# The products of the cosine transform between two halves of convolution 1's multiply-adds

## The chip, the core and the metric

The kernel runs as one program on one core of a Trainium2 chip. The core has a matrix engine (TensorE, "PE" in the profile, with its weight loads shown as "PEld"), a vector engine (VectorE, "DVE"), an engine for activations and copies (ScalarE, "ACT"), GpSimdE ("POOL", which here issues most DMAs and some memsets) and SyncE ("SP", which issues a few DMAs). Each engine works through its own list of instructions in order, and engines wait for each other through semaphores. The metric is the time of one execution in device microseconds.

## The reference

Two layers follow each other on eight images of 32 channels and 128 x 128 pixels. In layer 0 every pixel gets the eight best of 25 shifted copies of the normalised image, chosen by the squared difference summed over a patch. The stack of 256 channels goes through three pairs of a 1x1 convolution and a depthwise 3x3 convolution, and beside that through a small cosine transform (`dct`). The sigmoid of the third pair is multiplied with the transform, and two more 1x1 convolutions bring the product back to 32 channels. Layer 1 normalises again and convolves every channel with one 5x5 kernel.

```python
xb = _patch_match_stack(x)                       # [8, 256, 128, 128]
dct = _conv(xb, dct_w, groups=C)
h = jax.nn.relu(_conv(_conv(xb, w1), w2, groups=CK, pad=1))
h = jax.nn.relu(_conv(_conv(h, w3), w4, groups=CK, pad=1))
wiener = jax.nn.sigmoid(_conv(_conv(h, w5), w6, groups=CK, pad=1))
filt = _conv(wiener * dct, inv_dct_w, groups=C)
x = x + _conv(filt, agg_w)                       # layer 0, on the normalised x
x = x + conv5x5(_gn(x))                          # layer 1
```

## The kernel before

An image is worked through in 17 steps of eight rows (`NS` is 16, and the last step is short). The 256 channels are two halves of 128 partitions. For both halves TensorE does the 1x1 convolution. The depthwise part is split: the first half is done by TensorE with small diagonal weights (`depthwise_t`, tile `pw`, L751), the second half by VectorE as nine multiply-adds over shifted rows (`depthwise_v`). Of these nine, the first is a scaled copy on ScalarE (L722) and the other eight are instructions of VectorE, each `128x1024` (L725). ScalarE ends them with the ReLU or the sigmoid (L729).

The main loop goes over the steps `s`, and in each step over four passes `i` in the order 3, 2, 1, 0. Passes 3, 2 and 1 serve convolution 3, 2 and 1, each for another step (convolution 1 is the youngest). Pass 0 ends the step that convolution 3 has just finished: `final_dct` computes the cosine transform on TensorE into four PSUM tiles `pc` (L810, two pairs, one for rows 0 to 3 and one for rows 4 to 7) from the gathered stack `xf`, and VectorE multiplies them into the result of convolution 3 (L818, four products). In the next step's pass 3, `final_add` does the last 1x1 convolutions (`pa`, L831), VectorE adds the image (`xr`, L839), and GpSimdE issues the stores (`x1d`, L844).

TensorE, VectorE and ScalarE keep the order in which the program calls them (`manual_schedule` with `ORDERED`). `depthwise_v` is a generator, and each `next` on it issues one piece: the scaled copy; the eight multiply-adds; the activation; the move of the two border rows (`rows_before_v`, L655 and L657). The middle of a pass issues the multiply-adds of its own convolution with `next(new_v, None)` (L1094). The activation follows in the next pass with `next(dv, None)` (L1102), and the border rows in the pass after that (`next(kept, None)`, L1097). So in pass 1 VectorE does the eight multiply-adds of convolution 1, and the first thing that it does in pass 0 are the four products; then come the tasks that `tick` releases, and in pass 3 of the next step `xr` and the multiply-adds of convolution 3. ScalarE does convolution 1's ReLU in pass 0, behind the squares `df` that the tasks have brought, and before the first copies `tv` (L678) and the scaled copy L722 of convolution 3.

Tasks are the work on the next image and on layer 1. They are generators that name the engine they want next and a cost; `tick` hands out VectorE's by a budget per pass that is fixed in the program. The tasks of this page are: the differences `df` (L444, squared by ScalarE in L452, summed by TensorE into `pd`, L459), the search for the best eight, `mx` and `idx` (L536, L537), the places `oc` (L551 to L560, transposed by TensorE as `pi`, L569), the transposed costs `pt` and their copy `ct` (L525, L529), and layer 1's normalised rows `xm` (L897) with the matmuls on them (L924, called `p5` in the text, `p` in the profile).

PSUM tiles for the 1x1 convolutions (`pv` L670, `p` L694), `pg`, `pa`, `pc`, `pi`, `pt` and `p5` all come from one pool of five buffers (`ps_x`). A tile can be written only when the reader of its buffer's last tile is done: for `pc` that is the product on VectorE, for `pv` the copy `tv` on ScalarE, for `pa` the addition `xr` on VectorE, for `pg` the copy `xb` (L638) on ScalarE. Which buffer a tile gets, and the order of SyncE's and GpSimdE's instructions, is decided by the framework when the program is built, from its own estimate of when things end. The gather's selection masks `sel` (L616, L617) are ScalarE's.

Of the kernel before, what the change touches and what calls it, by code (L numbers as in the profile page):

```python
# [44 lines left out]
def bm3d_conv_preact(  # L45
# [165 lines left out]
    def push(task):  # L211
        want = next(task, None)
        if want:
            which, cost, *wait = want
            queues[which].append((cost, task, now[0] + (wait[0] if wait else 0)))
# [150 lines left out]
    def prep(b):  # L366

        xn = load_image(b, nc.gpsimd) if b else first
        yield "P", 0
        yield "D", 5.5  # L370
        st = work.tile([P, 8, 6], F32, name=f"st_{b}", tag="st")
        for i in range(8):
            nc.vector.bn_stats(
                st[:, i], xn[:, 3 + 4 * i : 7 + 4 * i, 2 : 2 + W]
            )
        mv = work.tile([P, 2], F32, name=f"mv_{b}", tag="mv")
        nc.vector.bn_aggr(mv, st.rearrange("p a b -> p (a b)"))
        yield "A", 0
        nc.scalar.copy(xn[:, :, 0:2], xn[:, :, 2:3].to_broadcast([P, HR, 2]))
        nc.scalar.copy(  # L380
            xn[:, :, 2 + W :], xn[:, :, 1 + W : 2 + W].to_broadcast([P, HR, 2])
        )
        mr = yield from group_stats(mv, f"a{b}")
        nc.vector.tensor_scalar(
            xn, xn, mr[:, 0:1], mr[:, 1:2], op0=ALU.subtract, op1=ALU.mult
        )
        push(sources(b, xn))

        idx = work.tile([P, 4, 8, K, 4], U32, name=f"idx_{b}", tag="idx", bufs=1)

        sq = dram.tile([NO // 2, 4, HR - 2, HX], F32, name=f"sq_{b}", tag="sq")
        for i in range((HR - 2) // SR):
            pd = ps_d.tile([P, SR // 2, HX], F32, name=f"pd_{b}_{i}", tag="pd")

            for aa in ((2, 4), (0, 0), (1, 1), (3, 2), (4, 3), (5, 5)):
                yield "D", PAIR
                push(squares(b, i, pd, xn, aa, sq, idx))
# [254 lines left out]
    def rows_before_v(i, b, n):  # L652
        v = tv[i - 1]
        if n < NS:
            nc.sync.dma_start(v[:, 0:2], v[:, R : R + 2])  # L655
        else:
            nc.gpsimd.memset(v[:, 0 : i + 1], 0.0)  # L657
# [53 lines left out]
    def depthwise_v(i, b, n):  # L711
        v = tv[i - 1]
        nr = R if n < NS else i
        out_ = accp.tile([P, R, W], F32, name=f"acc{i}_{b}_{n}_1", tag=f"acc{i}1")
        acc = out_[:, :nr]
        for k, (dy, dx) in enumerate(
            ((1, 1), (0, 0), (0, 1), (0, 2), (1, 0), (1, 2), (2, 0), (2, 1), (2, 2))
        ):
            tap = dwv[:, i - 1, 3 * dy + dx : 3 * dy + dx + 1]
            rows = v[:, dy : dy + nr, dx : dx + W]  # L720
            if k == 0:
                nc.scalar.activation(acc, rows, AF.Copy, scale=tap)  # L722
                yield out_
            else:
                nc.vector.scalar_tensor_tensor(  # L725
                    acc, rows, tap, acc, op0=ALU.mult, op1=ALU.add
                )
        yield
        nc.scalar.activation(acc, acc, funcs[i - 1])  # L729
        yield  # L730
        rows_before_v(i, b, n)
# [64 lines left out]
    def final_dct(b, n, acc, xf, j0, j1):  # L796

        for r0 in range(0, R, 4):
            a, z = max(r0, j0), min(r0 + 4, j1)
            if a >= z:  # L800
                continue


            pc = [
                ps_x.tile([P, 4, W], F32, name=f"pc_{b}_{n}_{m}_{r0}", tag="x") for m in range(2)
            ]
            for h in range(2):
                for m in range(2):
                    o = 64 * ((h + m + 1) % 2)
                    nc.tensor.matmul(  # L810
                        pc[m][o : o + 64, : z - a],
                        ldct[64 * h : 64 * h + 64, m],
                        xf[64 * h : 64 * h + 64, m, a:z],
                        start=True,
                        stop=True,
                    )
            for m in range(2):
                nc.vector.tensor_mul(acc[m][:, a:z], acc[m][:, a:z], pc[m][:, : z - a])  # L818
# [179 lines left out]
    def unit(stage, u, *rest):  # L998
        if 0 <= u < len(units) and units[u]:
            if stage is gather_load:  # L1000
                at = (units[u][0], units[u][1] % 8 // 2)
                until(lambda: at in ready, 4.0)
            stage(*units[u], *rest)
# [20 lines left out]
    def turn(credit):  # L1024
        now[0] += 1
        run("D", credit)
        run("A")
        run("P")
        run("Q")

    def until(cond, credit):
        while not cond():
            turn(credit)

    with tc.manual_schedule(engines=ORDERED):
        push(prep(0))
        push(weights())
        push(mixes())
        xbd[0] = dram.tile([P, 2, H, W], F32, name="xbd_0", tag="xbd")
        for i in range(3):  # L1040
            nc.gpsimd.memset(tb[i][0:64, 0], 0.0)
        for u in range(7):
            unit(gather_load, u)

            for _ in range({2: 3, 3: 1}.get(u, 0)):
                turn(4.0)
            unit(gather_select, u - 2)
            unit(gather_pixels, u - 3)
        u = 4

        dt = dv = kept = iter(())

        later = iter(())

        for s in range(len(steps) + 2):
            if s < len(steps):
                b, n = steps[s]
                if s == 2:
                    push(bands())
                if n == (0 if b else 4) and b + 1 < NB:  # L1060
                    until(lambda: b in ready, 4.0)
                    push(prep(b + 1))
                if n == NS - 1 and b + 1 < NB:
                    until(lambda: b + 1 in ready, 4.0)
                    xbd[b + 1] = dram.tile([P, 2, H, W], F32, name=f"xbd_{b+1}", tag="xbd")
            for i in (3, 2, 1, 0):
                si = s - (i - 1 if i else 2)
                live = 0 <= si < len(steps)
                new_v = new_t = iter(())
                if live:  # L1070
                    bi, ni = steps[si]

                if live and i:
                    src = source(i, bi, ni)
                    pointwise_v(i, bi, ni, lws[i - 1], src)
                    new_v, new_t = depthwise_v(i, bi, ni), depthwise_t(i, bi, ni)
                    accs[i, bi, ni] = [None, next(new_v)]
                next(later, None)
                if live and not i:
                    if ni == 0:  # L1080
                        x1d[bi] = dram.tile([C, H, W], F32, name=f"x1d_{bi}", tag="x1d")
                        stats[bi] = work.tile([P, NS + 1, 6], F32, name=f"stat_{bi}", tag="stat")
                    xr, xf, j0, j1 = fins.pop(si)
                run("P")
                if live and not i:
                    final_dct(bi, ni, accs[3, bi, ni], xf, j0, j1)

                run("Q")
                if s < len(steps):
                    unit(gather_select, u + 1, (0,))  # L1090
                    unit(gather_load, u + 3)
                    tick(b, i)
                next(later, None)
                next(new_v, None)  # L1094
                if live and i:
                    pointwise_t(i, bi, ni, lws[i - 1], src)
                next(kept, None)  # L1097
                if s < len(steps):
                    unit(gather_pixels, u)
                next(dt, None)  # L1100
                run("A")
                next(dv, None)  # L1102
                if s < len(steps):
                    unit(gather_select, u + 1, (1,))
                    u += 1
                next(dt, None)
                kept, dv, dt = dv, new_v, new_t
                if live and not i:
                    later = end(bi, ni, xr, j0, j1)
                if not i and 0 <= s - 1 < len(steps):  # L1110
                    fins[s - 1] = final_load(*steps[s - 1])
        next(kept, None)
        for _ in later:
            pass
        until(lambda: {(NB - 1, 0), (NB - 1, 1)} <= done, 4.0)
# [62 lines left out]
```

## Time and profile before

| | |
|---|---|
| median of 3 runs | 6632.68 us (6631.27 to 6632.92) |
| profiled execution | 6624.95 us |
| its span | 6623.2 us |
| mean granted TensorE clock | 0.98 |
| TensorE, VectorE, ScalarE busy | 94%, 89%, 76% of the span |
| one multiply-add of VectorE, 128x1024 | 1284 ns mean, 3072 of them |
| one product of VectorE, 128x512 | 680 ns mean, 496 of them |

The profile is of one execution, and all durations below are from it. A timeline row gives the start in microseconds from the span's start, the time that the row's instructions take together, the engine, the line of the program, the operation, the tiles (written from read), their shapes, the number of instructions, and in brackets the idle time of the engine just before with what ended it. A row of the list of waits gives who waited, behind whom, the total in microseconds, how often, and the longest. A wait for several things is put down to the one that came last.

### The profile page before, as it was taken

What the parts mean: (1) busy time and instruction counts of PE and PEld (TensorE: products, weight loads), DVE (VectorE), ACT (ScalarE), POOL (GpSimd) and SP (SyncE); (2) the same over time, 40 slices, a digit from 0 to 9 for tenths busy, and PEclk for the clock granted to TensorE, in tenths of its full rate; (3) what the DMA queues carried; (4) which work ended last, traced back from release to release, by engine and by line L of the source; (5) the groups of instructions that cost most, each with busy time, mean ns of one, the idle gap of its engine ahead of it and who ended that gap; (6) DMA issues with size and microseconds to landing.
All of it is one profiled execution on the core that took longest, in us unless ns stands there. A gap on an engine that the chain in (4) does not pass through costs nothing.

```text
span 6623.2 us, 234197 instructions
## 1 busy us (share of the span) xinstructions
PE 6230.9 (94%) x102306; PEld 3213.3 (49%) x102306; DVE 5861.9 (89%) x8828; ACT 5052.8 (76%) x6698; POOL 3083.0 (47%) x5015
## 2 busy tenths in 40 slices
PE   5898899999999999999999999999999999999997
PEld 1444455544554445544555544554445544465553
DVE  7899988999889998898989998899888999888786
ACT  5787778777787777877778877887768777687782
POOL 8354446444364343643446444464335543334334
PEclk8899999999999999999999999999999999999998
DMA  4555555655555564555645546465555555456553
GB/s 85 127 138 131 133 129 133 150 132 139 130 145 138 130 147 120 148 135 134 145 121 146 149 127 148 119 155 136 128 139 130 147 137 135 122 140 150 139 132 84
DMA packets 544959, 886.20 MB, mean 134 GB/s; under 512 B 248880, under 2 KB 312944, under 8 KB 543936
## 3 DMA queue, kind: packets, MB, share of 16 engines
q0 software_dynamic: 383648, 611.87, 36.8%
q1 hardware_dynamic: 157776, 258.11, 16.1%
q8 instruction: 805, 13.19, 0.9%
q10 hardware_dynamic: 2512, 1.25, 0.1%
q14 instruction: 218, 1.79, 0.1%
HBM read 420.60 MB, written 216.49 MB: 96 GB/s over the span
## 4 chain that ended last, share of the span: by engine, by line
PE 45%; DVE 29%; ACT 9%; DMA 6%; POOL 6%; issue 4%; SPq 0%; ACTq 0%; POOLq 0%; DVEq 0%
DVE acc L725 20%; PE pw L751 15%; PE pv L670 11%; PE p L694 10%; PE pg L631 4%; POOL xtd L424 2%; DVE idx L537 2%; PE pc L810 2%; ACT df L452 2%; ACT sel L616 2%; DVE df L444 2%; DMA xf<-xbd 1%; DVE acc L818 1%; DMA t<-t 1%; PE p L924 1%
## 5 line engine op out<-in xcount | busy, mean ns | idle before, releaser
L725 DVE SCALAR_TENSOR_TENSOR acc<-tv,dwv,acc 128x1024 f32<-128x1024 f32 (+3 forms) x3264 | 4032.3, 1237 | 237.7 <-ACT acc L722 133.7
L751 PE MATMUL pw<-t,dwd 96*32 96x254 f32 (+7 forms) x31680 | 2119.7, 419 | 23.3 <-DMA t<-t 15.2
L751 PEld LDWEIGHTS pw<-t,dwd 96*32 96x32 f32 (+1 forms) x31680 | 1079.7, 110 | 851.3 <-issue 386.1
L616 ACT ACTIVATE sel<-ib,nplace 128x1024 f32<-128x1024 uint8 x1024 | 1172.5, 1145 | 32.2 <-DMA ib<-idxd 32.2
L617 ACT ACTIVATE sel<-sel 128x1024 f32<-128x1024 f32 x1024 | 1085.9, 1060 | 32.5
L694 PE MATMUL p<-acc,lw 128*32 128x256 f32 x16768 | 1006.7, 383 | 26.5 <-ACT tv L678 26.5
L670 PE MATMUL pv<-acc,lw 128*32 128x512 f32 x8448 | 956.2, 590 | 52.0 <-DVE acc L818 46.7
L602 POOL DMA_DIRECT2D ib<-idxd x512 | 292.4, 571 | 1242.3 <-ACT sel L616 1186.9
L791 POOL DMA_DIRECT2D xf<-xbd x1088 | 652.6, 629 | 310.7 <-PE pc L810 176.1
L694 PEld LDWEIGHTS p<-acc,lw 128*32 128x32 f32 x16768 | 575.1, 112 | 444.4 <-issue 81.3
L452 ACT ACTIVATE df<-df 128x786 f32<-128x786 f32 (+2 forms) x576 | 468.6, 861 | 348.4 <-DVE df L444 345.8
L631 PE MATMUL pg<-sel,xt 120*32 120x88 f32 (+1 forms) x24576 | 618.8, 244 | 66.8 <-ACT sel L617 51.4
L631 PEld LDWEIGHTS pg<-sel,xt 120*32 120x32 f32 x24576 | 557.9, 111 | 238.4 <-ACT sel L617 69.9
L678 ACT COPY tv<-pv 128x512 f32<-128x512 f32 (+2 forms) x784 | 436.8, 580 | 296.6 <-PE pv L670 283.8
L444 DVE TENSOR_TENSOR df<-xn 128x786 f32<-128x786 f32 (+2 forms) x576 | 531.6, 973 | 86.0 <-PE pd L459 84.9
L729 ACT ACTIVATE acc<-acc 128x1024 f32<-128x1024 f32 (+3 forms) x408 | 417.3, 1023 | 240.8 <-DVE acc L725 240.5
L764 ACT ACTIVATE acc<-pw 128x512 f32<-128x512 f32 (+2 forms) x808 | 438.4, 573 | 167.2 <-PE pw L751 165.8
L670 PEld LDWEIGHTS pv<-acc,lw 128*32 128x32 f32 x8448 | 284.2, 111 | 538.8 <-issue 426.6
L701 ACT COPY t<-p 128x512 f32<-128x512 f32 x800 | 424.2, 572 | 119.8 <-PE p L694 119.7
L722 ACT ACTIVATE acc<-tv,dwv 128x1024 f32<-128x1024 f32 (+3 forms) x408 | 454.9, 1115 | 33.0 <-PE pa L831 19.1
L670 PE MATMUL pv<-xb,lw 128*32 128x512 f32 x4096 | 471.1, 593 | 0.0
L694 PE MATMUL p<-xb,lw 128*32 128x256 f32 x8192 | 468.1, 379 | 0.2 <-DVE xy L936 0.2
(155 smaller groups left out, 5923.1 us busy)
## 6 DMA issues: line engine op xcount, KB each, us to landing
ib<-idxd POOLq DMA_DIRECT2D x512, 256.0 KB, 4.1
xbd<-xb POOLq DMA_DIRECT2D x128, 1024.0 KB, 5.8
xf<-xbd POOLq DMA_DIRECT2D x960, 128.0 KB, 6.9
t<-t SPq DMA_DIRECT2D x792, 128.0 KB
t<-t SPq DMA_DIRECT2D x384, 256.0 KB
tv<-tv SPq DMA_DIRECT2D x384, 130.0 KB
xt<-xtd POOLq DMA_DIRECT2D x240, 180.0 KB, 3.8
xtd<-xl POOLq DMA_DIRECT2D x192, 96.0 KB, 3.4
```

Source lines behind the costliest of these rows:

```text
L444: nc.vector.tensor_sub(df[:, :, ca:cz], xn[:, r0 : r0 + SR, ca:cz], xn[:, r0 + dy : r0 + dy + SR, ca + dx : cz + dx],)
L452: nc.scalar.activation(df[:, :, ca:cz], df[:, :, ca:cz], AF.Square)
L616: nc.scalar.activation(sel, ib, AF.Square, bias=nplace)
L617: nc.scalar.activation(sel, sel, AF.Relu, scale=-1.0, bias=1.0)
L631: nc.tensor.matmul(pg[C * j : C * (j + 1), :, :, xa:xz], xt[: 8 * QW, f * (NT // 2) + t], sels[j // 2][: 8 * QW, j % 2 * 2 : j % 2 * 2 + 2 ...
L670: nc.tensor.matmul(ps[C * j : C * (j + 1), :hr], lhsT[:, g, P + C * j : P + C * (j + 1)], src(g)[:, h : h + hr], start=g == 0, stop=g == 1,)
L694: nc.tensor.matmul(ps[C * r : C * (r + 1), e, :nb], lhsT[:, g, s], rows[:, r : r + 4 * nb - 3 : 4], start=g == 0, stop=g == 1,)
L722: nc.scalar.activation(acc, rows, AF.Copy, scale=tap)
L725: nc.vector.scalar_tensor_tensor(acc, rows, tap, acc, op0=ALU.mult, op1=ALU.add)
L751: nc.tensor.matmul(pt[u][C * j : C * (j + 1), ka:kz, :nb, xa:xz], dwd[0:hi, i - 1, u, j, dx + 1], t[0:hi, j, ka:kz, :nb, xa + dx : xz + dx ...
L764: nc.scalar.activation(rows[:, u : u + 2 * nh[u] - 1 : 2, :nb], pt[u][:, : nh[u], :nb], funcs[i - 1])
L791: nc.gpsimd.dma_start(xf[p : p + C, m, j0:j1], src[g, m, (h + m + 1) % 2, :, :, ya:yz])
```

## The change

The eight multiply-adds of convolution 1 are issued in two pieces. The generator stops once more before the fifth of them, for convolution 1 alone, and pass 0 calls for the second piece right after `final_dct`. So VectorE's order becomes: four multiply-adds, four products, four multiply-adds. The order of TensorE's and ScalarE's instructions stays as it was. No instruction is added or removed.

```diff
@@ depthwise_v @@
                 nc.scalar.activation(acc, rows, AF.Copy, scale=tap)
                 yield out_
             else:
+                if i == 1 and k == 5:
+                    yield
                 nc.vector.scalar_tensor_tensor(
                     acc, rows, tap, acc, op0=ALU.mult, op1=ALU.add
                 )
@@ main loop @@
                 run("P")
                 if live and not i:
                     final_dct(bi, ni, accs[3, bi, ni], xf, j0, j1)
+                if not i:
+                    next(dv, None)
 
                 run("Q")
```

The taps are issued in the order (1,1), (0,0), (0,1), (0,2), (1,0), (1,2), (2,0), (2,1), (2,2), and `k` counts them from 0, so the second piece holds the last four.

## The prediction

> **What bounds the kernel now.** First the page's engines and the chain that ended last, then the list of waits, then timelines of single blocks.
>
> ```profile
> PE 6230.9 (94%) x102306; PEld 3213.3 (49%) x102306; DVE 5861.9 (89%) x8828; ACT 5052.8 (76%) x6698; POOL 3083.0 (47%) x5015
> ...
> PE 45%; DVE 29%; ACT 9%; DMA 6%; POOL 6%; issue 4%; SPq 0%; ACTq 0%; POOLq 0%; DVEq 0%
> ```
>
> No engine bounds it alone: the chain changes hands between TensorE and VectorE. The waits (microseconds in total, times, longest) name the hand-overs:
>
> ```profile
> ACT df L452 <- DVE df L444: 345.8, 89, 11.4
> ...
> ACT acc L729 <- DVE acc L725: 240.5, 91, 6.1
> DVE xr L839 <- PE pa L831: 228.4, 54, 8.1
> ...
> DVE acc L725 <- ACT acc L722: 133.7, 124, 4.7
> ...
> PE pv L670 <- DVE acc L818: 46.7, 25, 3.0
> ...
> PE p L694 <- ACT tv L678: 26.5, 12, 3.7
> ```
>
> TensorE's 46.7 us behind the products (L818) are what earlier products can free: `pv` waits for a PSUM buffer that `pc` holds. The 240.5 and 345.8 us are ScalarE waiting for VectorE: it serves in order, and behind those waits stand the `tv` copies and L722, which start convolution 3 on VectorE.
>
> Six of the eight images repeat one pattern of 17 blocks, some 805 us long; I read the one from 1064 to 1869. Two kinds of block matter. In the first, TensorE is late (timelines of VectorE, ScalarE and TensorE):
>
> ```profile
> 1362.96 5.25 DVE L725 SCALAR_TENSOR_TENSOR acc<-tv,dwv,acc 128x1024 f32<-128x1024 f32 x4
> 1368.13 2.47 DVE L818 TENSOR_TENSOR acc<-acc,pc 128x512 f32<-128x512 f32 x4
> ...
> 1381.25 3.93 DVE L725 SCALAR_TENSOR_TENSOR acc<-tv,dwv,acc 128x1024 f32<-128x1024 f32 x3 [1.62 <-ACT acc L722]
> ...
> 1373.28 1.74 ACT L452 ACTIVATE df<-df 128x786 f32<-128x786 f32 x2 [4.42 <-DVE df L444]
> ...
> 1365.16 1.95 PE L810 MATMUL pc<-xf,ldct 64*64 64x512 f32 x16
> ...
> 1379.60 3.66 PE L694 MATMUL p<-acc,lw 128*32 128x256 f32 x64 [0.79 <-ACT tv L678]
> ```
>
> The last four multiply-adds start at 1362.96, but `pc` is written from 1365.16 to 1367.1: today they cover that wait. In the second kind VectorE is late:
>
> ```profile
> 1669.54 2.47 DVE L818 TENSOR_TENSOR acc<-acc,pc 128x512 f32<-128x512 f32 x4
> ...
> 1676.08 6.57 DVE L725 SCALAR_TENSOR_TENSOR acc<-tv,dwv,acc 128x1024 f32<-128x1024 f32 x5 [0.35 <-ACT acc L722]
> ...
> 1669.66 1.06 ACT L729 ACTIVATE acc<-acc 128x1024 f32<-128x1024 f32 x1 [6.08 <-DVE acc L725]
> ...
> 1674.90 1.15 ACT L722 ACTIVATE acc<-tv,dwv 128x1024 f32<-128x1024 f32 x1
> ...
> 1670.28 3.64 PE L670 MATMUL pv<-acc,lw 128*32 128x512 f32 x32 [2.19 <-DVE acc L818]
> ```
>
> Here TensorE waits 2.19 us for the products, but ScalarE's ReLU L729 waits for the eighth multiply-add, and its chain ends in L722, for which VectorE waits.
>
> **The change part by part.** Nothing is added or removed: per block four multiply-adds (5.25 us in the row at 1362.96) change places with four products (2.47 us). Products come up to 5.2 us earlier; the eighth multiply-add 2.5 us later where `pc` is ready, more where it is not.
>
> *The wait removed.* TensorE's waits for L818 are 7.2 us per image at `pv`, and with `pc` and `pg` 46.7 + 7.8 + 3.6 + 0.8 = 58.9 us in all. Most are followed by a later wait on work that does not move: at 1521.8 `pv` waits 3.02 us, then `p` waits 3.67 us at 1533.6 for the `tv` copies, which stand behind VectorE's `df` (same time in both orders). There the stall only shifts. I count a gain at one block, 1669.
>
> *The wait added: products on `pc`.* Behind it on VectorE stand four multiply-adds, the paced tasks (`df`, `mx`, `oc`, `xm`), `xr` and convolution 3; behind those wait ScalarE's squares, L729 and all after them, and TensorE's `pd`, `p`, `p5`. Each half of `pc` takes about 1.0 us. Block by block:
> - 1271: `pc` starts at 1269.2, the four multiply-adds at 1265.7. VectorE waits 4.5 us and ends the group 4.7 us later. It absorbs 1.05 us (its wait for `pa`); ScalarE reaches L722 3.2 us later. In the next block TensorE's `p5` (L924) needs the `xm` that VectorE ends at 1327.7, right before `p5` starts at 1327.9: TensorE becomes late by the same. **+3.2.**
> - 1368: products at 1366.2 instead of 1368.1, four multiply-adds behind them, 3.35 us later in all; VectorE and TensorE both wait already on the chain through `df` (1.62 and 0.79 us above), so nothing absorbs it. **+3.35.**
> - 1418: 4.2 us later; a 2.8 us wait for `pa` absorbs part; L722 moves by 2.6. At 1471.5 TensorE waits for `df` and follows. **+2.6.**
> - 1621: `pc` is ready. L729 waits 5.41 us for the eighth multiply-add, now 2.45 us later; through L722 this reaches the copy `ct` L529, for which VectorE waits already (1.08 us at 1627.8). **+2.45.**
> - 1669: TensorE wins its 2.19 us, but `pg` behind it needs the PSUM buffer that the first `tv` copy frees 2.45 us later, and loses 0.85 again. VectorE's loss vanishes: from here to 1796 TensorE has no gap of 0.4 us. **−1.35.**
> - 1750: the products wait 1 us, L729 comes 3.4 us later, L722 2.4. VectorE runs without such a gap from it to ScalarE's waits at 1778.9 and 1800.9, and TensorE waits for `sel` at 1796. **+2.4.**
> - The other blocks: 0, hidden by VectorE's waits for `pa` (7.2 us at 1717.6) and `pd`, or by `pc` being ready with the same end of the group. Without that cover 1708 would cost 3.3, others up to 1.7.
>
> Sum 12.65 us per image, times six: 76 us. The last image is bound by TensorE:
>
> ```profile
> 6281.61 2.48 DVE L818 TENSOR_TENSOR acc<-acc,pc 128x512 f32<-128x512 f32 x4
> 6291.31 0.42 DVE L839 TENSOR_TENSOR xr<-xr,pa 128x256 f32<-128x256 f32 x1 [7.23 <-PE pa L831]
> ```
>
> VectorE idles 7.23 us after the products, more than the 3.3 us added; L729 would come 5 us later, but ScalarE's own gaps before the `tv` copies (1.1 us each) and after leave L722 about 1.5 us late, which TensorE does not feel. 0. The first image has four late `pc` (430, 651, 805, 901) of 1.7 + 3.2 + 1.3 + 3.4 = 9.6 us together and long waits elsewhere: between 0 and 9.6, I take 4.
>
> *Queues and buffers.* The schedule of SyncE and GpSimdE shifts by itself. On SyncE the DMA of `tv0` (L655) goes behind that of `t1` (L648) in many blocks; its reader, convolution 1's next `tv` copy, comes over 20 us later (1399.0 after the block of 1368): 0, and if the cover is gone at most the 2.5 us of the shift. On GpSimdE the memset L663, for which POOL waits 26.1 us until 1750.4, goes behind eight `xf` issues, one `ib` and four `x1d`, so to about 1760; its reader is a short L722 at 1774.5. The memset L657 goes from 1780.8 behind `x1d` to about 1797; its reader L722 starts at 1807.06. Both 0; without cover up to 9 us per image, while `xf` issued up to 4 us earlier could win some back: ends +54 and −24 us over six images, and I take 0 since both readers lie 10 us off. The PSUM pool hands out its five buffers in another order: in many blocks `p` now follows `pa` (freed by `xr`) instead of the first `tv` copy, worth 0.4 us at 1368 and at most 1.7 at 1521, where VectorE bounds: 0.
>
> Sum: 76 + 4 = 80 us on the profiled execution's 6624.95, so 6705; the median of the runs lies 7.7 us above it: 6713.
>
> *A rule weighed.* After the wait of 3.02 us at 1521.80 the 32 `pv` matmuls took 5.25 us, after 2.19 us (1670.28) 3.64; the granted clock was 0.69 from 1522 to 1527, and 1.00 from 1669 to 1676. The Trainium skill, "TensorE: Matmul & The Clock Gate", Part 1, says that TensorE falls to half its clock after an idle window of about 3.4 us and needs as long to recover. By this rule the change would remove one such stall per image and make up to two new ones (at `p5` near 1328, at `pd` near 1477): an estimate of 1.6 us more per image, about 6723. I keep to the row, since one stall goes where VectorE bounds.
>
> **The rivals.**
> 1. Faster: TensorE's 58.9 us of waits for L818 go and nothing takes their place, since the later stalls shrink with them: 6632.7 − 58.9 = 6574. For it: TensorE is 94% busy. Against it: `p` behind the 3.02 us stall waits on ScalarE, which does not move. It decides if VectorE's added wait stays under 7.4 us per image on the path (58.9 over eight images).
> 2. No change: the added waits fall into VectorE's 761 us of idle time and the removed ones come back at `p`: 6620 to 6646. For it: VectorE is idle 75 us in each such image. Against it: the rows at 1368, where both engines wait on the same chain.
> 3. Nothing absorbs: all delays of a middle image (1.7 + 4.7 + 0.9 + 3.35 + 4.2 + 1.1 + 3.3 + 1.0 + 2 × 2.45 = 25 us) and 3.3 us in each of 16 blocks of the last: 150 + 53 + 10 = 213, 6846. Against it: waits for `pa` up to 8.1 us.
>
> **How the numbers follow.** The forecast holds with 0.70, its own range 6660 to 6775 (from a third of the listed terms up to all of them, the first image's 9.6, and 7 us per image for 1708 and the small blocks uncovered); rival 1 has 0.11, rival 2 0.09, rival 3 0.10. The range 6625 to 6780 leaves out rival 1 and the upper part of rival 3. Within 0.2% (13 us), about what a measurement can tell from no change, lies rival 2 with 0.08; faster 0.11, slower 0.81.
>
> **What the changed profile would show.** The wait of L818 for `pc` rises from 13.1 us to over 80; `pv` on L818 falls from 46.7 to near 0; ScalarE's L729 on L725 rises from 240.5 us, by some 5 us in each late block of the last image alone; those blocks keep their 42.8 us; a middle image takes about 817 us instead of 804. Wrong it would be if `pc` came earlier with TensorE no longer stalled (the waits at 1271, 1368 and 1418 vanish), or if the reordered GpSimdE queue delays `ib` or `xf`.

## The result, and the profile after

The changed kernel takes 6750.0 us (median; 6747.5 to 6763.7), the kernel before 6632.8 beside it: a ratio of 1.018, with an interval of 1.0163 to 1.0198. The forecast was 6713 us with a range of 6625 to 6780. The profiled execution took 6747.5 us, its span is 6745.6, and its mean granted clock 0.972 instead of 0.980. The lines of the program have moved: L725 is now L727, L729 is L731, L751 is L753, L810 is L812, L818 is L820 and L839 is L841.

The page of the changed kernel, engines and chain:

```profile
PE 6285.5 (93%) x102306; PEld 3226.1 (48%) x102306; DVE 5855.3 (87%) x8828; ACT 5027.9 (75%) x6698; POOL 3073.1 (46%) x5015
...
PE 47%; DVE 29%; ACT 10%; DMA 5%; issue 4%; POOL 4%; ACTq 0%; DVEq 0%; SPq 0%; POOLq 0%
```

TensorE executes the same 102306 matmuls and is busy 54.6 us longer (6230.9 before). The slower granted clock is a part of that, and the sum of the forecast has no term for it. The list of waits of the changed kernel (total in us, times, longest):

```profile
ACT df L452 <- DVE df L444: 450.7, 95, 11.3
ACT acc L731 <- DVE acc L727: 448.4, 117, 8.1
...
DVE acc L820 <- PE pc L812: 205.1, 94, 6.0
DVE acc L727 <- ACT acc L722: 201.9, 109, 4.7
...
PE pi L569 <- DVE oc L560: 109.1, 25, 20.2
```

The products wait 205.1 us for `pc` (13.1 before), ScalarE's ReLU 448.4 us for the last multiply-add (240.5), the paced `df` squares 450.7 (345.8), and TensorE 109.1 us for `oc` (63.1). The removed wait is gone: `pv` had 46.7 us behind the products and now has no entry in the list.

The two blocks of the forecast's rows, in the changed kernel. First the one that stood at 1368, then the one at 1669 (timeline rows):

```profile
1379.16 1.95 PE L812 MATMUL pc<-xf,ldct 64*64 64x512 f32 x16
...
1380.35 2.48 DVE L820 TENSOR_TENSOR acc<-acc,pc 128x512 f32<-128x512 f32 x4 [3.44 <-PE pc L812]
...
1382.75 5.24 DVE L727 SCALAR_TENSOR_TENSOR acc<-tv,dwv,acc 128x1024 f32<-128x1024 f32 x4
...
1390.57 1.74 ACT L452 ACTIVATE df<-df 128x786 f32<-128x786 f32 x2 [7.72 <-DVE df L444]
```

```profile
1681.79 0.66 PE L569 MATMUL pi<-cst,oc 128*128 128x128 f32 x2 [4.43 <-DVE oc L560]
...
1682.38 3.69 PE L812 MATMUL pc<-xf,ldct 64*64 64x512 f32 x16
...
1692.70 3.60 PE L670 MATMUL pv<-acc,lw 128*32 128x512 f32 x32
...
1694.38 1.06 ACT L731 ACTIVATE acc<-acc 128x1024 f32<-128x1024 f32 x1 [6.01 <-DVE acc L727]
```

At 1368 it went as forecast: VectorE waits 3.44 us for `pc` (3.2 by the forecast, from 1362.96 to 1366.2), with four multiply-adds behind it, and ScalarE's wait for `df` grows from 4.42 to 7.72, by 3.3 (the sum had 3.35). At 1669 `pv` has no stall any more (2.19 us before), but `pi` ahead of it waits 4.43 us. Before, it waited 2.09:

```profile
1659.33 0.41 PE L569 MATMUL pi<-cst,oc 128*128 128x128 f32 x2 [2.09 <-DVE oc L560]
```

**Where the time came from.** Take the start of the first `pc` matmul of each image in both traces: the first image brings 4.6 us, the six middle images 107.5, the last one and the end some 10. For the middle images, the stretch from image 1's to image 7's first `pc`, before and then after (length, then TensorE's busy time, weight loads, VectorE, ScalarE, GpSimdE; then clock, DMA share, GB/s):

```profile
1112.70:5916.20 4803.50, 4624.00 (x76569) 2399.73 (x76568) 4347.71 (x6546) 3748.64 (x4971) 2256.57 (x3686) 0.99 0.55 137
```

```profile
1117.30:6028.30 4911.00, 4665.73 (x76569) 2401.38 (x76568) 4340.54 (x6544) 3734.34 (x4971) 2251.43 (x3686) 0.98 0.54 134
```

The length grows by 107.5 us, from 800.6 to 818.5 us for a mean middle image: 41.7 us of it is TensorE's busy time, for the same matmuls, and 65.8 its idle time. The forecast had 76 us for these images, all of it waits.

### The profile page after: what moved, and what is told of

It is laid out like the page before. It is cut to its first block, busy times and chain, and to the rows that moved or that the text cites. A ratio compares the mean times of both kernels' runs of the same rounds, so it can differ in the third digit from the quotient of the medians.

```text
span 6745.6 us, 234236 instructions
## 1 busy us (share of the span) xinstructions
PE 6285.5 (93%) x102306; PEld 3226.1 (48%) x102306; DVE 5855.3 (87%) x8828; ACT 5027.9 (75%) x6698; POOL 3073.1 (46%) x5015
## 4 chain that ended last, share of the span: by engine, by line
PE 47%; DVE 29%; ACT 10%; DMA 5%; issue 4%; POOL 4%; ACTq 0%; DVEq 0%; SPq 0%; POOLq 0%
DVE acc L727 18%; PE pw L753 16%; PE p L694 11%; PE pv L670 10%; PE pg L631 4%; DVE df L444 2%; PE pc L812 2%; ACT sel L616 2%; DVE idx L537 2%; DMA t<-t 2%; DVE acc L820 2%; PE p L926 2%; POOL xtd L424 2%; ACT df L452 2%; ACT acc L722 1%
## 5 line engine op out<-in xcount | busy, mean ns | idle before, releaser
L727 DVE SCALAR_TENSOR_TENSOR acc<-tv,dwv,acc 128x1024 f32<-128x1024 f32 (+3 forms) x3264 | 4030.5, 1237 | 304.2 <-ACT acc L722 201.9
L753 PE MATMUL pw<-t,dwd 96*32 96x254 f32 (+7 forms) x31680 | 2135.2, 421 | 53.5 <-DMA t<-t 28.8
L753 PEld LDWEIGHTS pw<-t,dwd 96*32 96x32 f32 (+1 forms) x31680 | 1082.8, 111 | 890.8 <-issue 413.5
L694 PE MATMUL p<-acc,lw 128*32 128x256 f32 x16768 | 1026.1, 386 | 22.1 <-DVE xr L841 13.4
L452 ACT ACTIVATE df<-df 128x786 f32<-128x786 f32 (+2 forms) x576 | 469.3, 862 | 453.6 <-DVE df L444 450.7
L731 ACT ACTIVATE acc<-acc 128x1024 f32<-128x1024 f32 (+3 forms) x408 | 416.9, 1022 | 448.6 <-DVE acc L727 448.4
L631 PE MATMUL pg<-sel,xt 120*32 120x88 f32 (+1 forms) x24576 | 633.6, 244 | 73.3 <-ACT sel L617 63.5
L820 DVE TENSOR_TENSOR acc<-acc,pc 128x512 f32<-128x512 f32 (+1 forms) x528 | 320.8, 665 | 205.2 <-PE pc L812 205.1
```

The source lines that it names most:

```text
L452: nc.scalar.activation(df[:, :, ca:cz], df[:, :, ca:cz], AF.Square)
L631: nc.tensor.matmul(pg[C * j : C * (j + 1), :, :, xa:xz], xt[: 8 * QW, f * (NT // 2) + t], sels[j // 2][: 8 * QW, j % 2 * 2 : j % 2 * 2 + 2 ...
L694: nc.tensor.matmul(ps[C * r : C * (r + 1), e, :nb], lhsT[:, g, s], rows[:, r : r + 4 * nb - 3 : 4], start=g == 0, stop=g == 1,)
L727: nc.vector.scalar_tensor_tensor(acc, rows, tap, acc, op0=ALU.mult, op1=ALU.add)
L753: nc.tensor.matmul(pt[u][C * j : C * (j + 1), ka:kz, :nb, xa:xz], dwd[0:hi, i - 1, u, j, dx + 1], t[0:hi, j, ka:kz, :nb, xa + dx : xz + dx ...
```

## The experiments

Every kernel is named by its run. The short diffs are against the changed kernel.

**Fewer and more multiply-adds behind the products (k8, k3).**

```diff
-                if i == 1 and k == 5:
+                if i == 1 and k == 8:      # k8: seven ahead, one behind; k3 has k == 3
```

> Seven multiply-adds ahead of the products, one behind (the change has four and four). Theory of the prediction (the products wait for pc, and all four multiply-adds behind them wait too): pc is ready when the seventh multiply-add ends in most blocks, 0.8 us are left at 1271 and 0.2 at 1418, so VectorE's wait for pc falls from 205.1 us to under 40; the ReLU stays behind the products, which keeps 2.45 us at 1621, 1.4 at 1750 and wins 0.45 at 1669: 6 x 4.35 = 26, about 6660 us. Rival, the late ReLU is the cost (ScalarE waits 448.4 us for it against 240.5): the eighth multiply-add stands behind the products all the same, so 6735 to 6750. Rival, the swap of orders in SyncE's and GpSimdE's queues costs the time wherever the products stand: 6735 to 6750.

> Two multiply-adds ahead of the products, six behind. Theory of the prediction: the products come 2.62 us earlier again, while pc does not; at the three late blocks (1271, 1368, 1418) and at 1750 all of that is added wait: 6 x 4 x 2.62 = 63 us on top of the changed kernel's 6750, so about 6813, and up to 20 more where blocks become late that are not yet (1321, 1572, 1708); the last image stays hidden (5.9 us of 7.2). Rivals, late ReLU or queue orders: the same ReLU and the same queues, so 6745 to 6760.

k8: 6647.9 us beside 6628.2, ratio 1.0032 (1.0019 to 1.0044), 20 us where 26 were expected. From its list of waits:

```profile
ACT acc L731 <- DVE acc L727: 387.2, 118, 7.8
...
DVE acc L820 <- PE pc L812: 33.8, 32, 3.2
```

ScalarE still waits 387.2 us for the late multiply-add, most of the 448.4, and yet five sixths of the cost are gone with the wait for `pc`. So the late ReLU is not the main cost. The swapped order of SyncE's queue is not tested by k8: of the 1560 copies of border rows that SyncE issues (L648, L655, L707, L709), one stands at another place than before in k8, and 124 in the changed kernel.

k3: 6945.9 us, ratio 1.0484 (1.0467 to 1.0502): 318 us, where some 180 to 200 were expected. The direction is that of the theory and not of its rivals, the size is not. The wait for `pc` is 433.5 us over 149 waits (94 in the changed kernel): many more blocks have become late than the `pc` times of the trace of before allow for. In the six middle images the length grows by 278.1 us, 103.7 of it in TensorE's busy time.

**The blocks apart (late3, rest).** The generator stops, and pass 0 calls, only where convolution 1's row block pairs with the products of the blocks 1271, 1368 and 1418; `rest` is the complement.

```diff
-                if i == 1 and k == 5:
+                if i == 1 and k == 5 and n in (5, 7, 8):        # rest: n not in (5, 7, 8)
...
-                if not i:
+                if not i and s < len(steps) and n in (5, 7, 8):
```

> The change at three of an image's 17 blocks alone, those where pc is latest (1271, 1368, 1418 in the image read). Theory of the prediction: 6 x (3.2 + 3.35 + 2.6) = 55 us by its own terms, 80 if all terms were too small in the measured proportion (107.5 instead of 76 in six images), and about 4 in the first image: 6690 to 6717. Rival, every block costs alike through queues or the clock: 3/17 of 117 us, 6653.

> The change at the 14 other blocks of each image. Theory of the prediction: 6 x (2.45 - 1.35 + 2.4) = 21 us, 38 if what the three late blocks leave is all here, and 4 to 10 for the first and the last image: 6655 to 6680. Rival, every block costs alike: 14/17 of 117 us, 6729. Rival, here TensorE's 58.9 us of waits are won and nothing is lost: below 6632.

late3: ratio 1.0111 (1.0095 to 1.0128), 72 us with three of 17 blocks. rest: 1.0054 (1.0036 to 1.0071), 32 us with fourteen. An equal share per block would be 21 and 96: the cost lies where `pc` is late. In SyncE's list 41 copies stand at another place than before in late3 and 89 in rest, and of GpSimdE's DMAs 51 and 91, so the swaps in the queues don't go with the cost.

The step of each block, worked out from the traces: by how much the start of its `pc` moves against before, from this block to the next, in us as a mean over the six middle images:

| block | forecast | late3 | rest | whole change |
|---|---|---|---|---|
| 1271 | 3.2 | 6.0 | 0.0 | 5.5 |
| 1321 | 0 | −0.6 | 1.5 | 1.5 |
| 1368 | 3.35 | 2.4 | −0.4 | 3.8 |
| 1418 | 2.6 | 3.6 | 0.2 | 4.6 |
| 1471 and 1521 | 0 | −1.4 | −2.0 | −3.2 |
| 1572 | 0 | 0.1 | 1.3 | 1.4 |
| 1621 | 2.45 | 0.0 | 2.4 | 2.4 |
| 1669 | −1.35 | −0.3 | −0.6 | −0.7 |
| 1708 | 0 | 0.0 | 0.0 | 0.0 |
| 1750 and 1782 | 2.4 | 0.2 | 2.5 | 2.5 |
| the others | 0 | −0.5 | −0.3 | 0.2 |
| an image | 12.65 | 9.5 | 4.4 | 17.9 |

The parts come close to the forecast: 9.5 against 9.15 for the three late blocks, 4.4 against 3.5 for the rest. The whole is 4 us per image more than its parts in these traces (24 us in six images; by the times it is 117 − 72 − 32 = 13 us). In the six images together the parts have 39.1 + 28.1 = 67.2 us of idle time of TensorE and 18.0 − 1.9 = 16.1 of longer busy time; the whole has 65.8 and 41.7. So in these traces, one execution each, the idle time adds up, and the excess is all in the busy time.

**Does the wait feed itself (late4, only4)?** The same edit with `n in (5, 6, 7, 8)`, and with `n == 6`.

> The change at four of 17 blocks: the three late ones and the one between them (1321). Measured so far: the three alone 72 us, the other fourteen 32 us, all seventeen 117; by trace some 15 us of the missing 13 to 25 arise between the blocks 1321 and 1418 of the six middle images (31.6 us there in the whole change, 10.8 with the three, 6.2 with the fourteen). Theory, the wait feeds itself: TensorE, made late at 1271, writes pc of 1321 late, a block whose pc is early in the trace of before, and the change adds a second wait there: 72 + 15 = 87 us, 6712 to 6725. By the prediction's own term for 1321, which takes pc's time from the trace of before: 0, so 6700. Rival, the missing part comes from queues or clock over the whole image: 6700 to 6704.

> The change at the block 1321 alone, in every image. With it and the three late blocks the ratio was 1.0130, with the three alone 1.0111. If the wait feeds itself, 1321 costs only where 1271 has made TensorE late; alone its pc is early, the added wait is 1.15 us and VectorE's next wait takes it up: 0 to 1 us per image, 6630 to 6640 (ratio 0.9995 to 1.0010). If the block has a cost of its own, the 2.4 us per image seen between the blocks 1321 and 1418 stay: 6648 or more (1.0022).

late4: ratio 1.0130 (1.0115 to 1.0146), 87 us. only4: 1.0012 (1.0003 to 1.0021), 8 us, just outside both expectations. By the times the question stays open: 87 − 72 = 15 us with the neighbours and 8 alone, both with some 6 to 15 us of uncertainty. The traces, one execution each, point to the neighbours: over the six middle images the step from 1321 to 1418 is 6.5 us in only4, 10.8 in late3 and 34.4 in late4. But the trace of late3 is of its fastest run (6.6 us below its median) and that of late4 of its slowest (4.8 above), so about half of the 24 us between these two may be the choice of the run. And of the 9.3 us that the trace of only4 is longer than that of before, 8.9 arise in the last image and behind it, and 2.4 in the six middle ones (the first is 1.9 shorter): its 8 us are no measure of 1321 there. This is the block 1321, before and then in the changed kernel:

```profile
1315.53 1.95 PE L810 MATMUL pc<-xf,ldct 64*64 64x512 f32 x16
...
1320.77 2.47 DVE L818 TENSOR_TENSOR acc<-acc,pc 128x512 f32<-128x512 f32 x4
```

```profile
1328.42 1.95 PE L812 MATMUL pc<-xf,ldct 64*64 64x512 f32 x16
...
1329.61 2.48 DVE L820 TENSOR_TENSOR acc<-acc,pc 128x512 f32<-128x512 f32 x4 [4.26 <-PE pc L812]
```

Before, its `pc` began at 1315.53 and was done long before its products at 1320.77. In the changed kernel it begins 12.9 us later (4.6 of them are from before this image), and VectorE waits 4.26 us for it, where the times of the trace of before would give some 1.15 (the expectation of only4): the forecast read `pc` from that trace and took it as fixed. That the wait feeds itself fits late4 and this row; by the times it is not shown.

**The last image (last).** The same edit with `b == NB - 1 and n > 1`.

> The change in the last image's 17 blocks alone. The prediction's term: 0, VectorE has 7.23 us of idle time after the products: 6628 to 6633. By the shift of the matmuls of pc in the traces (8.3 us at three blocks of that image in the changed kernel, 7.1 with the three late blocks): the blocks near 6104 to 6196 are not of the steady 42.8 us kind and cost 6 to 9: 6635 to 6641.

6636.8 us beside 6633.8, ratio 1.0004 (0.9995 to 1.0013). The time can't tell 0 from 6 us. In the trace `pc` is 0.7 us late up to the block 6104 and 10.7 us from the block 6196 on, where it stays for eight blocks. So the steady blocks are hidden, as forecast. How much the two between cost is not clear: in the trace of win (below), whose edit leaves these two alone, `pc` falls back by 3.0 us over them as well.

**An earlier `pc` (early_before, early_after, half).** `final_dct` is cut: the matmuls of its first two PSUM tiles are issued in pass 1, before convolution 2's depthwise matmuls.

```diff
+            if r0 == 0:
+                yield                      # half: yield before both pairs of products
             for m in range(2):
                 nc.vector.tensor_mul(acc[m][:, a:z], acc[m][:, a:z], pc[m][:, : z - a])
...
-                    final_dct(bi, ni, accs[3, bi, ni], xf, j0, j1)
+                    for _ in dct:              # half: the first products, next(dv, None), the rest
+                        pass
...
+                if i == 1 and 0 <= s - 2 < len(steps):
+                    dct = final_dct(*steps[s - 2], accs[(3, *steps[s - 2])], *fins[s - 2][1:])
+                    next(dct)
                 next(dt, None)
```

> Kernel before, with the eight first matmuls of pc of each block issued ahead of convolution 2's depthwise matmuls on TensorE, so that pc is ready some 6 us earlier; two of five PSUM buffers are held that much longer. Nothing on VectorE waits for pc before, so a change comes only from PSUM buffers or from xf's transfers: 6615 to 6650. It is the yardstick for the next run.

> The changed kernel with the same earlier matmuls of pc. Theory (the products' wait for a late pc, and its feeding of itself, is the cost): VectorE's wait for pc falls from 205 us to under 50, and of the 117 us stays the ReLU part, 6 x (2.45 - 1.35 + 1.4) = 15, give or take 15: 0 to 30 us above the run early_before. Rival, the late ReLU or the queue orders are the cost: 90 to 117 us above early_before.

> First pair of pc's PSUM tiles written ahead of convolution 2's depthwise matmuls as in the two runs before; on VectorE four multiply-adds, the two products of that pair, four multiply-adds, the two products of the second pair. In the run early_after only the first pair was early, and the 200.7 us of waits for pc stood before the second pair. Theory (the wait for pc with multiply-adds behind it is the cost): the wait falls to under 20 us, the ReLU comes 1.24 us later: at most 6 x 1.24 = 8 us above early_before's 6635 and, if TensorE wins part of its 42 us behind the products, down to 6620. Rivals: late ReLU as the cost, half of the delay, half of the 117 us: 6690; queue orders: 6735.

early_before: ratio 1.0003 (0.9994 to 1.0012), a neutral yardstick. early_after: 1.0173 (1.0157 to 1.0188), no better than the change, against the theory as I had put it. The list of waits says why:

```profile
DVE acc L822 <- PE pc L812: 200.7, 77, 5.9
```

The wait did not go. The first products find their `pc` ready; the second pair of `pc` is still written at the old place, and VectorE waits there, with the same four multiply-adds behind it. I had moved only half of the matmuls. In half, the second two products go back behind the multiply-adds, and TensorE's order is that of early_after:

```profile
ACT acc L731 <- DVE acc L727: 224.3, 93, 6.2
...
DVE acc L821 <- PE pc L812: 6.9, 4, 4.7
```

half: ratio 1.0005 (0.9996 to 1.0014). With the wait for `pc` down to 6.9 us the 107 us of early_after above early_before are gone, although two products still stand between the multiply-adds. Half alone doesn't separate the causes: ScalarE's wait for the late multiply-add falls as well (397.5 us in early_after, 224.3 here), and SyncE's list is nearly that of before again (8 copies at another place, 129 in early_after). But k8 kept that wait of ScalarE at 387.2 us and cost 20 us, and k3, with nearly the SyncE list of the changed kernel (23 copies moved against it), costs 318. Taken together, not the place in the middle costs, but waiting there for something that is not ready.

**The two blocks where TensorE waited for the products (win).** The same edit with `n in (10, 13)`, the blocks 1521 and 1669.

> The change at the two blocks alone where TensorE waits longest for the products (1521: 3.02 us, 1669: 2.19 us) and pc is long written. The prediction's term: 0 at 1521, where the stall only shifts, and -1.35 us at 1669: 6 x 1.35 = 8 us faster, 6626 (ratio 0.9988). Rival 1 of the prediction: both waits are won, 6 x 5.2 = 31 us: 6602. By the trace of the fourteen blocks, where the step over 1669 was +2.4 us in every middle image and not a gain: 6640 to 6648, if that step belongs to 1669 and not to the late ReLU of 1621, which is left out here.

6617.1 us beside 6627.1, ratio 0.9985 (0.9976 to 0.9994): 10 us faster, where 8 were forecast for these blocks and 31 by rival 1. It is faster than both kernels, by little. The steps over 1471 to 1521 are −2.2 us per image and over 1669 −1.6, and 1572 and 1621 give back 1.4 and 1.2. So the agreement of 10 with 8 is in part luck: 1521 was forecast at 0 and wins, and the losses at 1572 and 1621 were not forecast. At 1521 the stall shifts; before, and then in win:

```profile
1521.80 5.25 PE L670 MATMUL pv<-acc,lw 128*32 128x512 f32 x32 [3.02 <-DVE acc L818]
...
1533.60 6.17 PE L694 MATMUL p<-acc,lw 128*32 128x256 f32 x64 [3.67 <-ACT tv L678]
```

```profile
1519.23 3.61 PE L670 MATMUL pv<-acc,lw 128*32 128x512 f32 x32
...
1526.97 0.66 PE L569 MATMUL pi<-cst,oc 128*128 128x128 f32 x2 [3.26 <-DVE oc L560]
...
1532.39 5.43 PE L694 MATMUL p<-acc,lw 128*32 128x256 f32 x64 [1.34 <-DVE xr L841]
```

The 3.02 us at `pv` are gone, `pi` behind it waits 3.26 for `oc`, and `p` waits 1.34 instead of 3.67.

**The border rows (noxf).** In the changed kernel TensorE stalls in the block after 1271. Timeline rows, before and then changed:

```profile
1288.49 2.37 SPq L709 DMA_DIRECT2D t<-t  x1
...
1296.54 5.37 PE L751 MATMUL pw<-t,dwd 96*32 96x256 f32 x96
```

```profile
1294.73 0.46 SPq L707 DMA_DIRECT2D t<-t  x1
...
1295.25 2.51 SPq L709 DMA_DIRECT2D t<-t  x1
...
1301.78 2.78 PE L753 MATMUL pw<-t,dwd 96*32 96x256 f32 x46
...
1308.89 5.32 PE L753 MATMUL pw<-t,dwd 96*32 96x256 f32 x48 [4.33 <-DMA tv<-tv]
```

The second half of `pw` needs border rows that the DMA at 1295.25 (L709) copies within `t`. By the record of its semaphore that DMA landed at 1308.85, just before `pw` went on (the releaser in the bracket is another transfer of that moment). Before, the same DMA landed at 1298.63, 10.1 us after its issue began; now it is issued 6.8 us later, behind ScalarE's later copies to `t`, and takes 13.6. Over the six middle images such waits over 0.8 us, in the blocks after 1271 and after 1418, are 32.4 us (for 12 of them the profile names no releaser); before 1.4, in late3 32.0, in rest 0. In noxf the transfers of `xf` are left out:

```diff
+        if xfs:
+            return xr, xfs[0], j0, j1
         xf = xbp.tile([P, 2, R, W], F32, name=f"xf_{b}_{n}", tag="xf", bufs=1)
+        xfs.append(xf)
```

> The changed kernel with the transfers of xf left out after the first (every block multiplies the same eight rows, so the output is another; TensorE, VectorE and ScalarE do the same work). In the changed kernel TensorE waits 32.4 us in the six middle images, in the blocks that follow 1271 and 1418, for the border rows of t (1.4 us in the kernel before); in one of them the copy L709 landed 13.6 us after its issue began, in the kernel before 10.1. Between 1295 and 1312 there, 1.0 of 2.7 MB moved are xf's. Theory, the rows land late because they share the DMA engines with such transfers: the landing falls to 7 to 9 us, these waits to under 12 us, the time to 6715 to 6735. Rival, ScalarE's late t copies alone make the rows late, and the landing does not matter: waits of 25 to 33 us, 6744 to 6756. VectorE's waits for pc are untouched by either (some 200 us).

6707.3 us, ratio 1.0122 (1.0105 to 1.0139), where the change alone has 1.018. The same place in noxf:

```profile
1294.43 0.46 SPq L707 DMA_DIRECT2D t<-t  x1
...
1294.95 2.42 SPq L709 DMA_DIRECT2D t<-t  x1
...
1304.66 2.79 PE L753 MATMUL pw<-t,dwd 96*32 96x256 f32 x48 [0.41 <-DMA t<-t]
```

L709 begins at nearly the same time, lands after 9.7 us (a little more than the 7 to 9 expected), and `pw` waits 0.41 us. The waits in the two blocks fall from 32.4 to 8.0 us; 9.1 us of the same kind turn up after 1368. VectorE still waits 190.0 us for `pc`. So the landing matters, and the late copies alone don't explain the stall. In the trace of noxf the step over 1271 is 2.9 us and over 1418 1.1 (5.5 and 4.6 in the changed kernel), and the six middle images are 78 us longer than before, not 107.5. What the kernel before would win without these transfers was not run, so the 38 us between 1.018 and 1.0122 can't all be put down to the border rows.

## Why the prediction was right, and where it was not

The direction, the range and the mechanism held: the products wait for `pc`, everything behind them on VectorE comes later, and little is won for it.

- **The wait removed.** Right in the main. `pv` no longer waits for the products, and most of the stall shifts: `pi` waits 109.1 us instead of 63.1. It does not shift whole at 1521: the step over 1471 and 1521 is −3.2 us in the changed kernel and −2.2 in win, where 0 was forecast. That win came out at 10 us for 8 is in part luck, as said there. In the whole change the step at 1669 is −0.7 instead of −1.35.
- **The wait added, block by block.** The sum was 12.65 us per middle image; alone, the two groups of blocks measure 9.5 and 4.4. 1621 (2.45 against 2.4) and 1750 (2.4 against 2.5) are right. 1271 was mis-sized, 3.2 against 6.0 alone and 5.5 in the whole: the path I followed led through `xm` to `p5`, and the one that ended last led through ScalarE's copies to `t` and their border rows. At 1418 the forecast's reading is off: at 1471.5 TensorE waits 0.76 us for the products, and its wait for `df`, 0.74 us, ends at 1477.5; the step was 3.6 and 4.6 instead of 2.6.
- **"The other blocks: 0".** Wrong at 1321, by the traces: its cover, a `pc` that is ready early, was gone in the changed kernel, most likely through the delay at 1271. k3 fits this, with more work behind the wait and 149 waits for `pc` instead of 94. 1572 costs 1.4 us that were not forecast, and 1471 and 1521 win 3.2, so a part of the errors cancels.
- **"Queues and buffers: 0".** The step failed by what it left out. It weighed the order of `tv0` and `t1` in SyncE's queue, and not the DMAs of `t` itself (L707, L709), whose slack was small: the rows landed at 1298.63, and `pw`, then running since 1296.54 without a break, needed them in its second half. These stalls are 31 us (32.4 less 1.4) beside TensorE's 65.8 us of added idle time. Whether they stand in for delays that the 76 us already count, or come on top, is not settled: in noxf, with most of them gone, the middle images are close to the forecast (78 us), but the kernel before was not run without those transfers.
- **"A rule weighed … I keep to the row".** This term was the wrong one to put at 0: TensorE's busy time grew by 41.7 us in the six middle images, where the forecast fell short by 31.5. Not all of it is the clock. The traces' record of the granted clock holds 1.0 and 0.5 and nothing else; TensorE's busy time at 0.5 is 99 us of these images before and 153 after. Matmuls take nearly twice as long there (below), so the clock's part is an estimate of half the difference, 27 us. The clock does not explain the other 15; 10 of them are in the matmuls of `pd`. The forecast's argument, that one stall goes where VectorE bounds, counted stalls near three places and left out the others. The trace shows such a place (stretches; TensorE's busy time first, the granted clock third from the end):

```profile
1304.00:1308.00 4.00, 0.56 (x10) 0.08 (x2) 3.93 (x4) 3.60 (x5) 2.01 (x4) 1.00 0.90 180
1308.00:1314.00 6.00, 5.11 (x51) 2.39 (x55) 5.82 (x6) 0.60 (x1) 4.81 (x8) 0.54 0.65 197
```

  After the 4.33 us stall at 1308.89 the clock is 0.54, and 48 matmuls of `pw` take 5.32 us (2.79 in noxf). After the 4.43 us at 1681.79 the clock is 0.50 from 1682 to 1686, and `pc` takes 3.69 us (2.17 in this block before). The Trainium skill, "TensorE: Matmul & The Clock Gate", Part 1, has the rule that an idle window of about 3.4 us halves the clock; these two rows agree with it. It spoke in the right direction, with an estimate of 1.6 us per image where 27 us in six images are 4.5. Shorter stalls count here too: from 1100 to 6300 us in the traces of before and after, all 22 stalls of TensorE of 3.25 us or more that began at the full clock were followed by half the clock within 3.5 us, and so were 26 of the 49 from 2 to 3.25 us. No run took the throttle away, so this is an account by TensorE's time, not a cost shown by itself.
- **First and last image.** 4 forecast and 4.6 measured for the first. For the last, the steady blocks keep their 42.8 us as forecast, and two earlier ones bring 6 to 10 us in the traces (6.4 in the changed kernel, 7.2 in late3, 10.0 in last) where 0 was forecast; 3 of them also stand in the trace of win, which leaves these two blocks alone.
- **The range.** The terms that the upper end of the forecast's own range names, 76 + 9.6 + 42 us, give 6760 and not 6775; the measured 6750 lies below both.
- **The rivals.** Rival 1 (all 58.9 us won) fell with win: two of the longest stalls give 10 us, not 31. Rival 2 (no change) fell with the 117 us; only where `pc` is ready does the time stay (half). Rival 3 (nothing absorbs, 6846) is not reached with four multiply-adds behind the products; with six (k3) the time lies beyond it.

What stays open: how far 1321 costs by itself and whether the wait feeds itself there, what the border rows add to the forecast's terms, and whether the 27 us would be gone on a steady clock. The last two overlap, since stalls for border rows are also followed by a slow clock.

## What to carry to other kernels

Work put ahead of other work on an in-order engine must be ready by then: read when its input is written, and count everything behind it as delayed by the wait. Those times are not fixed: where the delayed engine feeds the one that writes the input, the next block's input is late too, so walk the chain round once more before calling a block covered. And give a new stall of TensorE two prices, the idle time and the slower clock after it (here `pc` took 3.69 instead of 2.17 us behind a stall of 4.43).

## What the hardware showed that I had not expected

The copies of border rows, 128 KB within SBUF, take 4.0 us in the median from issue to landing (L709), the slowest tenth over 7.5 and one 14.0; with the transfers of `xf` left out the tenth begins at 5.9 us and the median is 3.6. The total for L709 hardly differs between the kernels (1804 us before, 1792 after): in sum the copies did not become slower, and only some of them, at another moment of issue, landed later.
